# Adding gathered expert rows back: later additions for the last blocks, seven places, one rank at a time

## The chip, the cores and the metric

The kernel runs on one core of a Trainium2 chip. Its time is the device time of one execution in microseconds; before the change three runs gave a median of 1987.5 us (1986.58 to 1990.99). Engines are called by their names in the profile: PE (TensorE), PEld (TensorE's weight loads), DVE (VectorE), ACT (ScalarE), POOL (GpSimd) and SP (SyncE, which here only issues transfers).

## The reference

Two layers of cross attention and a feed-forward part run over 32 x 64 = 2048 tokens of width 512, in 32-bit floats. The change lies in the very last part, the feed-forward part of the second layer. Cut down to it:

```python
logits = x @ W_gate + b_gate                     # 8 experts
_, top_idx = jax.lax.top_k(logits, 2)
y_all = jax.nn.relu(jnp.einsum('bsd,edh->bseh', x, W_e) + b_e)   # x: layer-normed
y = jnp.take_along_axis(y_all, top_idx[..., None], axis=2)
out = x_before_norm + y.mean(axis=2)
```

Each token goes to its two best experts; the mean of the two results is added to the token.

## The kernel before

All instructions stand in one program whose order per engine is made by a scheduler from dependences, except where `pin` keeps the written order. Every engine executes its own instructions in order, and a transfer is issued by an engine's queue in order too: loads and stores of the result by SP, stores of y by ACT, gathers by POOL.

The 2048 tokens are four chunks of 512 (`NC = 4`), and each chunk is four tiles of 128 tokens (`TT = 4`), 16 tiles in all. Behind the attention, the normalised rows have been scattered into lists per expert in device memory (`xg`). The lists are worked off in blocks of 128 rows: `NB = 39` blocks, of which the first `FULL = 17` hold no row of the last chunk, and the first `COVER = 31` hold all rows of the first three chunks.

The last loop runs over `m` from 0 to 39. Round m turns block m (`block_turn`, L1445: four transposes on PE and a copy on ACT, L1447) and multiplies block m - 1 with its expert's weights (`block_expert`, products at L106). Then DVE adds the bias (L1466) out of the PSUM bank, of which there are two for these products, ACT applies Relu with a factor of one half (L1467) and stores the block's 128 rows of 512 to `yg` in device memory (L1468). The rows of a block are loaded by `load_rows` (L1426 reads a register with the place, L1431 loads), four blocks to one tile of the `t8` ring, which has four places; the last tile holds blocks 37 and 38.

From round 31 on the way back begins. `send_back(c, t)` issues two gathers (L1474, indirect transfers on POOL): for each token of tile t of chunk c its row of rank 0 and its row of rank 1, out of `yg` into a place `ys` of 2 x 512 values per partition. Five such places lie in the `weights` tile. Odd rounds send one tile, even rounds two, so the 12 tiles of the first three chunks are sent in rounds 31 to 38. These gathers need the first 31 blocks; those of the last chunk need all 39.

`combine(c, t, ys)` adds the two gathered rows (L1483), adds the sum to the tile of x (L1484), both on DVE and pinned, and stores the tile as result (L1485, SP). Odd rounds from 33 on combine one tile, even rounds two, up to round 38, which makes nine tiles (0 to 8). In a round the combine stands behind the bias addition of block m - 1. After the loop each of the last chunk's four tiles is sent, with one combine after each send, and then the rest is combined. Tiles are numbered 0 to 15 below in the order in which they are sent.

Of the kernel before, what the change touches and what calls it, by code (L numbers as in the profile page):

```python
# [12 lines left out]
ALU = mybir.AluOpType  # L13
# [16 lines left out]
def layers(ctx: ExitStack, tc: tile.TileContext, a: dict, out: bass.AP):  # L30
    nc = tc.nc
# [40 lines left out]
    def t8(name):  # L72
        return pools["work"].tile([P, 4, 512], F32, tag="t8", name=name, bufs=bufs["t8"])
# [25 lines left out]
    def pin(ins):  # L99
        return tc.keep_in_program_order(ins)  # L100
# [9 lines left out]
    weights = xpool.tile([P, 2, 5120], F32, tag="weights", name="weights")  # L110
# [182 lines left out]
    COVER = (2 * FIRST + NE * (P - 1)) // P  # L293
    NB = (2 * T + NE * (P - 1)) // P
# [491 lines left out]
    for i in range(len(order) + 1):  # L786
# [53 lines left out]
        p, step = divmod(i, 4)  # L840
# [341 lines left out]
    def attn1_out(k, oT, halves):  # L1182

        for i in halves:
            pp = ps_mm(f"pp_{k}_{i}")[:, 0:256]
            ss = slice(256 * i, 256 * i + 256)
            accumulate_next(pp, [(oT[:, j, :], wo1[:, j, ss]) for j in range(4)])
            x = xs[k][:, ss]
            nc.vector.tensor_tensor(x, pp, x, ALU.add)
# [76 lines left out]
    def route_row(c, h, at, t, r):  # L1266
        ins = pin(
            nc.gpsimd.indirect_dma_start(
                out=xg,
                out_offset=bass.IndirectOffsetOnAxis(ap=at[:, r, t : t + 1], axis=0),  # L1270
                in_=h[:, t, :],
                in_offset=None,
            )
        ).ins
        for other in sum(scatters.values(), []):
            tc.declare_no_dep(ins, other, reason="rows of a list are distinct")
        if c == NC - 1:
            for load in full_loads:
                tc.declare_no_dep(ins, load, reason="rows of full blocks are others")
        for clearing in clearings:  # L1280
            tc.add_manual_dep(ins, clearing.name, waits, reason="cleared before")
        scatters[c].append(ins)
# [138 lines left out]
    def load_rows(j0, j1):  # L1421

        base = 0 if j0 < FULL else FULL
        xr = t8(f"xr_{j0}")
        for j in range(j0, j1):
            v = nc.values_load(  # L1426
                tables[base][0:1, 1, j - base : j - base + 1], engines=[mybir.EngineType.SP],
                min_val=0, max_val=NE * T - P,
                skip_runtime_bounds_check_because="an expert's list and a block within it",
            )  # L1430
            load = nc.sync.dma_start(xr[:, j - j0, :], xg[bass.ds(v, P), :]).ins  # L1431
            for c in range(NC):
                for ins in scatters[c]:
                    if j < FULL and c == NC - 1:
                        tc.declare_no_dep(load, ins, reason="rows of full blocks are others")
                    else:
                        tc.add_manual_dep(load, ins.name, waits, reason="all rows are written")
            if j < FULL:
                full_loads.append(load)
        return xr  # L1440

    def block_turn(j, xr):
        pt = ps_tr(f"px_{j}").rearrange("p (k n) -> p k n", k=KT)
        for k in range(KT):
            pin(nc.tensor.transpose(pt[:, k, :], xr[:, k * P : (k + 1) * P], ident))  # L1445
        xT = t2(f"xT_{j}").rearrange("p (k n) -> p k n", k=KT)
        nc.scalar.copy(xT, pt)  # L1447
        return xT

    def block_expert(j, xT):  # L1450
        base = 0 if j < FULL else FULL
        v = [
            nc.values_load(
                tables[base][0:1, 0, j - base : j - base + 1], engines=[e],
                min_val=0, max_val=NE - 1,
                skip_runtime_bounds_check_because="a count of lists, less than NE",
            )
            for e in (mybir.EngineType.PE, mybir.EngineType.DVE)
        ]
        py = ps_mm(f"py_{j}")  # L1460
        flat = arena.rearrange("p e k n -> p (e k) n")
        accumulate_next(
            py, [(xT[:, k, :], flat[:, bass.ds(v[0] * KT + k, 1), :]) for k in range(KT)]
        )
        y = t2(f"y_{j}")
        pin(nc.vector.tensor_tensor(y, py, be1[:, bass.ds(v[1], 1), :], ALU.add))  # L1466
        nc.scalar.activation(y, y, AF.Relu, scale=0.5)  # L1467
        nc.scalar.dma_start(yg[j * P : (j + 1) * P, :], y)  # L1468

    def gather(c, t, at, ys):  # L1470

        slots_of = COVER if c < NC - 1 else NB
        for r in range(2):
            nc.gpsimd.indirect_dma_start(  # L1474
                out=ys[:, r, :],
                out_offset=None,
                in_=yg[0 : slots_of * P, :],
                in_offset=bass.IndirectOffsetOnAxis(ap=at[:, r, t : t + 1], axis=0),
            )

    def combine(c, t, ys):
        x = xs[c * TT + t]
        pin(nc.vector.tensor_tensor(ys[:, 0, :], ys[:, 0, :], ys[:, 1, :], ALU.add))  # L1483
        pin(nc.vector.tensor_tensor(x, x, ys[:, 0, :], ALU.add))  # L1484
        nc.sync.dma_start(out[(c * TT + t) * P : (c * TT + t + 1) * P, :], x)  # L1485

    for k in range(KT):
# [17 lines left out]
    def route_step(c, step):  # L1505
        n = f"e{c}"
        if step in ("rows0", "rows2"):
            t0 = int(step[-1])
            if t0 == 0:
                prep["h"] = route_rows if c < NC - 2 else t8(f"h_{n}")  # L1510
            stats = row_stats([xs[c * TT + t0 + i] for i in range(2)], f"{n}_{t0}")
            for i in range(2):
                norm_row(c, t0 + i, stats, prep["h"][:, t0 + i, :], i)
        elif step in ("turn0", "turn2"):
            t0 = int(step[-1])
            if t0 == 0:
                prep["fT"] = route_T if c < NC - 2 else t8(f"fT_{n}")
            for t in (t0, t0 + 1):
                turn_row(t, prep["h"][:, t, :], prep["fT"], n)
        elif step == "logits":  # L1520
            prep["parts"] = route_parts(c, prep["fT"])
        elif step == "ranks":
            prep["keep"] = route_keep(c, prep["parts"])
        elif step == "places":
            at = route_places(c, prep["keep"])
            sends.extend((c, prep["h"], at, t, r) for t in range(TT) for r in range(2))
# [99 lines left out]
    assert not sends  # L1626
    xr, turned, waiting, back = {}, None, [], 0

    def send_back(c, t):
        nonlocal back  # L1630
        ys = weights[:, 1, back % 5 * 1024 : (back % 5 + 1) * 1024]
        back += 1
        ys = ys.rearrange("p (r n) -> p r n", r=2)
        gather(c, t, slots[c], ys)
        waiting.append((c, t, ys))

# [7 lines left out]
    for m in range(NB + 1):  # L1644
        xT = turned
        if m < NB:
            if loads and loads[0][0] == m:
                j0, j1 = loads.pop(0)
                rows_m = load_rows(j0, j1)
                xr.update({j: rows_m[:, j - j0, :] for j in range(j0, j1)})  # L1650
            if m == 0:
                attn1_out(NC * TT - 1, oTs.pop(NC * TT - 1), (0, 1))
            turned = block_turn(m, xr.pop(m))
        if m > 0:
            block_expert(m - 1, xT)
        for step in between.get(m, ()):
            route_step(NC - 1, step)
        for _ in range(2):
            if sends:
                route_row(*sends.pop(0))  # L1660
        if m == 9:
            tables[FULL] = close_rest()
        elif m > 16 and m - 17 < NC:
            slots[m - 17] = token_rows(m - 17)
        if m >= COVER and left:
            for _ in range(2 - m % 2):
                if left:
                    send_back(*left.pop(0))
        for _ in range(2 - m % 2 if COVER + 2 <= m < NB else 0):
            combine(*waiting.pop(0))  # L1670
    assert not sends and not left
    for t in range(TT):
        send_back(NC - 1, t)
        combine(*waiting.pop(0))
    while waiting:
        combine(*waiting.pop(0))

# [53 lines left out]
```

## Time and profile before

| what | us |
|---|---|
| median of three runs | 1987.5 |
| the profiled execution | 1988.88 |
| its span, first to last instruction | 1987.0 |
| PE busy in the span | 1888.4 |
| DVE busy | 1056.9 |
| POOL busy | 548.3 |
| gathers (L1474), all 32: first and last start | 1930.5 and 1977.8 |
| one gather on POOL, median | 0.954 |
| from a gather's issue to its landing, least, median, most | 3.3, 5.1, 6.4 |
| one addition at L1483 or L1484 on DVE | 0.69 |
| store of a result tile to its landing, least, median, most | 2.0, 4.2, 6.8 |

In the rows of the order in time, the first number is the start in us from the span's start, the second the duration, then the engine (with a q: its queue), the line, the operation, what is written <- what is read, and in brackets how long the engine had been idle and what ended it. A row of the table of windows has the stretch, its width, then for PE, PEld, DVE, ACT and POOL the busy time and number of instructions, then the granted clock of PE (1.00 is full), the busy share of the 16 DMA engines and their GB/s.

### The profile page before, as it was taken

What the parts mean: (1) busy time and instruction counts of PE and PEld (TensorE: products, weight loads), DVE (VectorE), ACT (ScalarE), POOL (GpSimd) and SP (SyncE); (2) the same over time, 40 slices, a digit from 0 to 9 for tenths busy, and PEclk for the clock granted to TensorE, in tenths of its full rate; (3) what the DMA queues carried; (4) which work ended last, traced back from release to release, by engine and by line L of the source; (5) the groups of instructions that cost most, each with busy time, mean ns of one, the idle gap of its engine ahead of it and who ended that gap; (6) DMA issues with size and microseconds to landing.
All of it is one profiled execution on the core that took longest, in us unless ns stands there. A gap on an engine that the chain in (4) does not pass through costs nothing.

```text
span 1987.0 us, 26632 instructions
## 1 busy us (share of the span) xinstructions
PE 1888.4 (95%) x10544; PEld 1545.4 (78%) x10544; DVE 1056.9 (53%) x2077; ACT 519.9 (26%) x1019; POOL 548.3 (28%) x581
## 2 busy tenths in 40 slices
PE   7999999999998799999999999999999999879993
PEld 5888988889887698998998987787777776655441
DVE  6455445445546754454454456455466466663415
ACT  2211212212212222122122122311221565543221
POOL 7221121121322211211211211141344535540115
PEclk9999999999999899999999999999999999989997
DMA  9992110111210101111110012000004201214628
GB/s 330 307 301 89 39 43 33 33 43 40 67 43 11 43 33 32 43 32 33 43 32 22 22 59 88 19 1 11 0 22 138 64 12 54 85 71 133 217 94 271
DMA packets 129882, 151.72 MB, mean 76 GB/s; under 512 B 4704, under 2 KB 84384, under 8 KB 129760
## 3 DMA queue, kind: packets, MB, share of 16 engines
q1 hardware_dynamic: 118752, 122.70, 19.5%
q0 software_dynamic: 5392, 17.11, 2.6%
q10 hardware_dynamic: 5616, 10.23, 1.4%
q8 instruction: 84, 1.38, 0.3%
q14 instruction: 38, 0.31, 0.1%
HBM read 92.60 MB, written 56.36 MB: 75 GB/s over the span
## 4 chain that ended last, share of the span: by engine, by line
PE 88%; DVE 6%; DMA 2%; ACT 2%; issue 1%; POOL 1%; POOLq 0%; SPq 0%; DVEq 0%; ACTq 0%
PE ppx_o L464 11%; PE pqx_a L464 9%; PE sc_a L106 6%; PE pqz_a L464 6%; PE ppz_o L464 6%; PE py L106 6%; PE po_o L106 3%; PE pp L106 3%; PE pdx_f L464 3%; PE pqv_a L464 3%; PE ppy_o L464 3%; PE pqy_a L464 3%; PE px_v L554 2%; PE phx_f L464 2%; PE px_k L554 2%; PE pq_b L106 2%
## 5 line engine op out<-in xcount | busy, mean ns | idle before, releaser
L405 ACT ACTIVATE at_a<-at_a 128x512 f32<-128x512 f32 x64 | 40.4, 631 | 444.0 <-DVE at_a L404 444.0
L106 PE MATMUL py<-arena,xT 128*128 x312 | 140.8, 593 | 0.4 <-ACT xT L1447 0.2
L633 ACT ACTIVATE u_a<-pqx_a,bq 128x256 f32<-128x256 f32 x192 | 80.6, 471 | 163.4 <-PE pqx_a L464 161.1
L464 PE MATMUL ppx_o<-weights,oT_o 128*128 128x256 f32 x512 | 122.8, 383 | 0.1
L464 PE MATMUL pqz_a<-arena 128*128 128x256 f32 x512 | 121.0, 379 | 0.0
L464 PE MATMUL pqx_a<-arena,weights 128*128 128x256 f32 x512 | 121.0, 379 | 0.0
L106 PEld LDWEIGHTS sc_a<-kv,qT_a 128*128 128x128 f32 x1024 | 119.4, 192 | 1.7
L106 PE MATMUL sc_a<-kv,qT_a 128*128 128x64 f32 x1024 | 117.9, 273 | 0.0
L729 DVE TENSOR_TENSOR x<-ppx_o,x 128x512 f32<-128x512 f32 x128 | 86.9, 679 | 46.5 <-PE ppx_o L464 44.6
L464 PEld LDWEIGHTS pqz_a<-arena 128*128 128x128 f32 x512 | 97.2, 190 | 13.6 <-issue 0.4
L641 DVE TENSOR_TENSOR qT_a<-pqz_a,u_a 128x512 f32<-128x512 f32 x64 | 44.3, 692 | 113.9 <-ACT u_a L633 81.1
L464 PEld LDWEIGHTS pqx_a<-arena,weights 128*128 128x128 f32 x512 | 94.9, 190 | 12.0 <-DMA arena<-in_ctxT 0.2
L464 PEld LDWEIGHTS ppx_o<-weights,oT_o 128*128 128x128 f32 x512 | 94.8, 190 | 12.0 <-ACT oT_o L719 0.5
L106 PEld LDWEIGHTS py<-arena,xT 128*128 128x128 f32 x312 | 56.1, 190 | 56.5 <-issue 56.0
L446 POOL TENSOR_TENSOR arena<-weights 128x512 f32<-128x512 f32 x15 | 19.1, 1272 | 270.3 <-PE ppz_o L464 270.3
L436 POOL TENSOR_TENSOR arena<-weights 128x512 f32<-128x512 f32 x17 | 21.8, 1286 | 204.0 <-PE pqz_a L464 200.9
L436 POOL TENSOR_TENSOR kv_room<-weights 128x256 f32<-128x256 f32 x14 | 10.7, 762 | 238.6 <-DMA weights<-in_Wkv 238.6
L641 DVE TENSOR_TENSOR qT_a<-pqy_a,u_a 128x512 f32<-128x512 f32 x32 | 22.1, 692 | 101.5 <-PE pqy_a L464 101.5
L1466 DVE TENSOR_TENSOR y<-py,weights 128x512 f32<-128x512 f32 x39 | 26.9, 691 | 85.0 <-PE py L106 77.2
L403 DVE TENSOR_REDUCE mx_a<-sc_a 128x8 f32<-128x512 f32 x64 | 44.3, 692 | 44.3 <-PE sc_a L106 44.3
L106 PE MATMUL po_o<-atT_o,kv 64*128 64x256 f32 x512 | 65.9, 392 | 0.8 <-ACT atT_o L698 0.8
L1015 POOL TENSOR_TENSOR s_f<-s_f,arena 128x512 f32<-128x512 f32 x16 | 21.5, 1361 | 157.0 <-DVE s_f L1012 117.1
(427 smaller groups left out, 4264.9 us busy)
## 6 DMA issues: line engine op xcount, KB each, us to landing
xg<-zero SPq DMA_DIRECT2D x8, 4096.0 KB, 20.1
weights<-in_Wq SPq DMA_DIRECT2D x16, 1024.0 KB, 5.3
weights<-in_Wo SPq DMA_DIRECT2D x16, 1024.0 KB, 5.3
xr<-xg SPq DMA_DIRECT2D x39, 256.0 KB, 3.5
yg<-y ACTq DMA_DIRECT2D x39, 256.0 KB, 2.2
weights<-in_Wkv SPq DMA_DIRECT2D x16, 512.0 KB, 3.4
arena<-in_W_e SPq DMA_DIRECT2D x8, 1024.0 KB, 6.1
x<-in_x SPq DMA_DIRECT2D x16, 256.0 KB, 8.3
```

The source lines that it names most:

```text
L106: nc.tensor.matmul(ps, lhsT, rhs, start=(i == 0), stop=(i == len(pairs) - 1))
L403: nc.vector.tensor_reduce(mx, p3, AX.X, ALU.max)
L405: nc.scalar.activation(dst, dst, AF.Exp, scale=scale)
L436: engine.tensor_tensor(s1, a21, a22, ALU.add)
L446: engine.tensor_tensor(t1, b12, b11, ALU.subtract)
L464: nc.tensor.matmul(ps[:, m, :], left[:, k, m * P : (m + 1) * P], right[:, k, :], start=first and m == i == k == 0, stop=i == len(pairs) - ...
L554: nc.tensor.matmul(out_ps, *sides, start=first and m == k == 0, stop=k == 1, skip_group_check=True,)
L633: nc.scalar.activation(u[:, m * 256 : (m + 1) * 256], ps[:, m * 256 : (m + 1) * 256], AF.Identity, bias=bq[:, 4 * g + 2 * heads + m : 4 * ...
L641: nc.vector.tensor_tensor(q5[:, heads, :, 4 * half : 4 * half + 4, :], ps.rearrange("p (m b q) -> p m b q", m=2, q=64), u.rearrange("p (m ...
L729: nc.vector.tensor_tensor(dst, ps.rearrange("p (m n) -> p m n", m=2), dst, ALU.add)
L1015: nc.gpsimd.tensor_tensor(y, y, gamma, ALU.mult)
L1466: pin(nc.vector.tensor_tensor(y, py, be1[:, bass.ds(v[1], 1), :], ALU.add))
```

## The change

Three things change, all on the way back. The combines of rounds 37 and 38 leave the loop, and behind the loop all but three of the waiting tiles are combined ahead of the last chunk's gathers; the last chunk's four tiles are then sent without a combine between them. Gathered rows get seven places instead of five: two more lie in a tile of the `t8` ring, taken when the sixth tile is sent. And `combine` adds each rank's rows to x in an instruction of its own instead of adding the two ranks first.

```diff
     def combine(c, t, ys):
         x = xs[c * TT + t]
-        pin(nc.vector.tensor_tensor(ys[:, 0, :], ys[:, 0, :], ys[:, 1, :], ALU.add))
-        pin(nc.vector.tensor_tensor(x, x, ys[:, 0, :], ALU.add))
+        for r in range(2):
+            pin(nc.vector.tensor_tensor(x, x, ys[:, r, :], ALU.add))
         nc.sync.dma_start(out[(c * TT + t) * P : (c * TT + t + 1) * P, :], x)
...
+    homes = [weights[:, 1, i : i + 1024] for i in range(0, 5120, 1024)]
+
     def send_back(c, t):
         nonlocal back
-        ys = weights[:, 1, back % 5 * 1024 : (back % 5 + 1) * 1024]
+
+        if back == 5:
+            two = t8("ys").rearrange("p i n -> p (i n)")
+            homes.extend(two[:, i : i + 1024] for i in (0, 1024))
+        ys = homes[back % 7].rearrange("p (r n) -> p r n", r=2)
         back += 1
-        ys = ys.rearrange("p (r n) -> p r n", r=2)
         gather(c, t, slots[c], ys)
         waiting.append((c, t, ys))
...
-        for _ in range(2 - m % 2 if COVER + 2 <= m < NB else 0):
+
+        for _ in range(2 - m % 2 if COVER + 2 <= m < NB - 2 else 0):
             combine(*waiting.pop(0))
     assert not sends and not left
+    while len(waiting) > 3:
+        combine(*waiting.pop(0))
     for t in range(TT):
         send_back(NC - 1, t)
-        combine(*waiting.pop(0))
     while waiting:
         combine(*waiting.pop(0))
```

In the order that the scheduler makes of it, the loads of blocks 37 and 38 move behind the first store of a result tile in SP's queue, and the three bias additions of blocks 36 to 38 follow each other on DVE without an addition of gathered rows between them.

## The prediction

> **What bounds the kernel now.** I read the page first, for the stage that the change touches, then the rows of that stage in order of time, then the waits and the landing times behind them.
>
> ```profile
> span 1987.0 us, 26632 instructions
> PE 1888.4 (95%) x10544; PEld 1545.4 (78%) x10544; DVE 1056.9 (53%) x2077; ACT 519.9 (26%) x1019; POOL 548.3 (28%) x581
> ```
>
> TensorE fills the span, but the change only touches what follows it: the way back, where gathered rows are added to x. The table of windows over that stage:
>
> ```profile
> 1897.00:1930.00 33.00, 33.00 (x105) 16.34 (x104) 5.80 (x9) 8.92 (x16) 0.00 (x0) 1.00 0.23 83
> 1930.00:1957.00 27.00, 26.54 (x77) 12.23 (x75) 15.49 (x23) 7.72 (x13) 20.73 (x20) 1.00 0.86 288
> 1957.00:1987.00 30.00, 0.00 (x0) 0.00 (x0) 11.67 (x17) 0.63 (x1) 12.33 (x13) 0.55 0.70 231
> ```
>
> TensorE (first figure after the width) is done at 1957; the last 30 us hold none of it. This tail is what can shrink. VectorE, in order of time:
>
> ```profile
> 1956.26 0.69 DVE L1484 TENSOR_TENSOR x<-x,weights 128x512 f32<-128x512 f32 x1
> 1959.49 0.69 DVE L1483 TENSOR_TENSOR weights<-weights 128x512 f32<-128x512 f32 x1 [2.53 <-DMA weights<-yg,at_r]
> 1960.21 0.69 DVE L1484 TENSOR_TENSOR x<-x,weights 128x512 f32<-128x512 f32 x1
> 1960.82 0.68 DVE L1466 TENSOR_TENSOR y<-py,weights 128x512 f32<-128x512 f32 x1
> ...
> 1982.39 0.69 DVE L1483 TENSOR_TENSOR weights<-weights 128x512 f32<-128x512 f32 x1 [0.97 <-DMA weights<-yg,at_r]
> 1983.12 0.69 DVE L1484 TENSOR_TENSOR x<-x,weights 128x512 f32<-128x512 f32 x1
> ```
>
> The bias addition of the last block (L1466 at 1960.82) stands behind the ninth tile's combine, which waited 2.53 us for its rows. The block's product was ready long before:
>
> ```profile
> 1953.06 3.67 PE L106 MATMUL py<-arena,xT 128*128 x8 [0.19 <-DVE y L1466]
> ```
>
> It ends at 1956.73. GpSimd, whose queue issues all gathers:
>
> ```profile
> 1959.88 1.13 POOL L1474 DMA_INDIRECT weights<-yg,at_r  x1 [0.30 <-issue]
> 1961.31 0.95 POOL L1474 DMA_INDIRECT weights<-yg,at_r  x1 [0.30 <-issue]
> 1968.33 0.95 POOL L1474 DMA_INDIRECT weights<-yg,at_r  x1 [6.07 <-DVE x L1484]
> ...
> 1977.79 0.95 POOL L1474 DMA_INDIRECT weights<-yg,at_r  x1 [0.30 <-issue]
> ```
>
> Its queue is full from 1930.48 to 1962.26, idle for 6.07 us, then full again with the eight gathers of the last chunk. Those need every row of yg, so also block 38's. The row blames an addition, but the addition that this gather needs for its place (tile 7's) ended at 1956.95. The real releaser is block 38's store: issued at 1962.20, its landing is
>
> ```profile
> DMA to landing us min/median/max: 5.3/5.3/5.3
> ```
>
> so 1967.5, and the gather starts 0.83 us later. The path of the end is thus: y of block 38 (1960.82), Relu and store issue (1962.20), landing (1967.5), eight gathers (1968.33 to 1977.79), landing of the last (4.5 us, 1982.3), two additions (1983.81), the last store and the end (3.2 us, 1987.0).
>
> **Part 1: additions of blocks 36 to 38 ahead of the combines.** The combines of rounds 37 and 38 (tiles 6, 7, 8) move behind y of block 38; tile 9's and the later ones stand behind them in the same order as before. No instruction is added or removed. y of block 36 still stands behind the combine of tile 5: its second row was issued at 1944.78 and took 5.9 us, so 1950.7; one addition of 0.69 us instead of two, so y of 36 at about 1951.5 (1952.22 before), and the 0.19 us hold of block 38's product goes: it would end at 1956.5. I do not count these 0.2 us, for the reason in part 2, and put y of block 38 at 1956.73 + 0.1 = 1956.8: **4.0 us** earlier. Relu and issue keep their 1.38 us: the store leaves at 1958.2.
>
> Its landing: stores of y took 2.0 us while nothing else moved and 4.3 to 5.7 us since the gathers began. Here a rule of the Trainium skill bears ("DMA: Bandwidth & Descriptors", section "Queues, rings and completion order"): each DMA engine takes turns between the queues that have work, by packets. So the store, on ScalarE's own queue, would not stand behind a backlog of the others but pay for how many of them are busy. After the change no tile is stored between about 1952.5 and 1959.0 (two stores left in that time before, at 1954.39 and 1956.98), so SP's queue should be nearly empty when the store starts. By the row of the same store the landing is 5.3, by the rule it is between 2.0 and 4.3 while only the gathers share. From 1959.0 on, tiles 6, 7 and 8 follow each other at 1.4 us with a store each, so the cover is short: I take 5.0, nearest the rows (ends 4.3 and 5.7). It lands at 1963.2; with the 0.83 us the first gather starts at 1964.0, **4.3 us** earlier.
>
> Is GpSimd free by then? Tiles 9 to 11's gathers end at 1962.26 now. Two costs: the combines of tiles 6, 7, 8 are now back to back (six times 0.72, 1957.6 to 1961.9) beside four gathers. The rows: a gather takes 0.95 us undisturbed, and 1.13 to 1.47 where additions run beside it (1951.51: 1.47). The rule speaks against the change more strongly ("SBUF — State Buffer", "Who interferes with whom"): a VectorE instruction with two inputs in SBUF, as every one of these additions, contends with a GpSimd instruction that reads SBUF, and the loser of the port blocks for the other's whole length; the page infers that writing descriptors alone is spared. Taken at its worst that is 0.69 us a gather, 2.8 us for four, and GpSimd free at 1965.0, one microsecond too late. By the rows it is four times 0.35, free at 1963.7, just under the store's landing. I take the rows; the rule's end is in the range.
>
> **Part 2: seven places.** Gathers 5, 6, 12 and 13 go to a new tile of the t8 ring. Places: tile 12 needs tile 5's combine, 13 tile 6's, 14 tile 7's (done about 1960.4), 15 tile 8's (1961.9), all ahead of 1964. So part 1 can put the combines back without stalling the gathers; with five places tile 12 would have had to wait for tile 7. Before tile 11 the places cost nothing: GpSimd's idle time before gathers was 0.3 us each, its own issue.
>
> The ring has four places, and the new tile takes one. The loads of blocks 37 and 38 (last of the ring) now wait for block 28's transposes instead of block 24's, and in SP's queue they now stand behind the first store of the result, as the listing of the program's order shows. What is moved, then, is two loads of 256 KB:
>
> ```profile
> 1895.25 1.16 SPq L1431 DMA_DIRECT2D xr<-xg  x2
> 1938.05 0.35 SPq L1485 DMA_DIRECT2D out<-x  x1
> ...
> 1944.96 0.60 PE L1445 MATMUL px<-ident,xr 128*128 128x128 f32 x4
> ```
>
> They were issued at 1895, in quiet; now behind a store at about 1937.4 (one addition earlier than 1938.05), so at 1938.2 and 1939.0 (0.83 us apart, as in back-to-back loads). Loads of this kind landed in 2.6 to 4.5 us; stores and gathers at 1938 to 1943 took 3.8 to 6.4. With 5.5 block 37's rows are there at 1943.7, needed by the transposes at 1944.96: 1.2 us to spare, block 38's (1944.5 against 1948.83) have 4. I price this at zero, hidden under the products of blocks 34 and 35; without that cover each microsecond past 1944.96 is a microsecond on the end, because block 38's product follows. At 6.4 nothing is lost yet. The 0.52 MB also come into a stretch where the DMA engines are 0.9 to 1.0 busy at about 340 GB/s: 1.5 us of their time, partly in the gaps before 1942 (shares of 0.84 to 0.91). Gathers of tiles 3 to 5 may land some 0.3 to 0.6 us later and with them y of 36, whose slack is 0.7: hence the 0.2 us that I left out above.
>
> **Part 3: each rank by itself.** Still 32 additions of 0.69 us, on the same bytes. The first now waits only for the first row. Behind the last gather one addition stands instead of two: 1.42 becomes 0.69 (with its gap), **0.7 us** off the end. Elsewhere it is hidden.
>
> **The sum.** First gather of the last chunk at 1964.0 (-4.3). Eight gathers took 9.46 us from first to last start, with two stretched ones; tiles 9 to 11 are added until about 1967, so I add one stretch of 0.35: last start at 1973.8. Landing 4.5 as before (the stores of tiles 12 and 13 beside it, as now): 1978.4; one addition, 1979.15; 3.2 us to the end: 1982.35. That is some 4.6 us off the profiled span of 1987.0, whose execution took 1988.88 in all. The median of the runs is 1987.5, so **1982.9**.
>
> **Rivals.**
> - *The transfers keep most of it.* From 1942 to 1966 the DMA engines are full. If the store takes 5.7, the last gathers run into the stores of tiles 9 to 11 (0.7 more), additions stretch three gathers more than I count (1.05), and the loads are late by a little, the gain is about 2.2: 1985.3. For it: the shares near 1.0; against: 0.5 to 0.8 from 1967 on, and two stores moved later.
> - *The places do nothing, only part 3 pays.* If the first gather did wait for the addition that its row names (1968.00) and the new order kept such an addition ahead of it: 1986.8. Against: the place's addition was over at 1956.95, and the landing fits.
> - *Slower: blocks 37 and 38 are late.* Their loads stand behind the first store. Each microsecond past 1944.96 costs one; the gain is used up with a landing at 1949.6, and the time is over by 0.2% with one past 1953.6. At 1955 it would be about 1993. The longest landing of the stretch is 6.8 us, that is 1945.0; so it needs something that no row shows.
>
> **How the numbers follow.** A change of 0.2% is about what a measurement of this kernel tells from no change, 4.0 us here: faster means below 1983.5. The likeliest case (1982.9) has 0.63, most but not all of it below that line, the kept transfers 0.26, part 3 alone 0.05, late blocks 0.06. Faster 0.58 (0.05 of the likeliest case falls short of the line), same 0.35, slower 0.07 (0.01 for part 3 alone with a little lost besides). Range: low by y of 38 at 1956.6 (-4.2), landing 4.3 (-1.0), no stretches (-0.66), a last landing of 3.8 (-0.7) and -0.7: 7.3 off, 1980.2. High by the kept transfers and half the case of part 3 alone, with the median's own spread: 1987.0.
>
> **What would show it.** Right: y of block 38 at about 1956.8 directly behind its product; the idle time ahead of the last chunk's gathers down from 6.07 to about 1 to 2 us; their first at 1964; a single addition behind the last landing. Wrong: an idle TensorE at block 37's or 38's transposes, released by a load; gathers of 1.3 us and more in a row from 1957 on; a landing of block 38's store near 6 us; or the end set by another tile's rows.

## The result

The changed kernel takes 1982.69 us (median of eight runs, 1980.77 to 1987.3) against 1987.95 us before (median of eight runs). The ratio is 0.9973, with an interval from 0.9962 to 0.9984: 5.4 us saved, somewhere between 3.2 and 7.6. The forecast was 1982.9. The profiled execution took 1984.12 us, its span is 1982.2 us, 4.8 less than the 1987.0 of before.

The page and the windows over the way back, after the change (windows: stretch, width, then PE, PEld, DVE, ACT and POOL with their busy time and count, then granted clock, busy share of the DMA engines, GB/s):

```profile
span 1982.2 us, 26637 instructions
PE 1889.5 (95%) x10544; PEld 1546.5 (78%) x10544; DVE 1054.9 (53%) x2077; ACT 520.0 (26%) x1019; POOL 548.1 (28%) x581
```

```profile
1930.00:1957.00 27.00, 26.28 (x76) 12.13 (x74) 13.13 (x21) 7.68 (x13) 20.54 (x21) 1.00 0.90 313
1957.00:1987.00 30.00, 0.00 (x0) 0.00 (x0) 13.42 (x21) 0.63 (x1) 12.15 (x12) 0.59 0.66 226
```

TensorE has the same work and ends 0.45 us earlier (1956.28 against 1956.73); GpSimd issues the same gathers. What is shorter is the tail behind TensorE: the span ends at 1982.2, so the last window holds only 25.2 us of it, where it held 30.0. VectorE in order of time, after the change:

```profile
1949.52 0.69 DVE L1484 TENSOR_TENSOR x<-x,ys 128x512 f32<-128x512 f32 x1
1950.67 0.69 DVE L1484 TENSOR_TENSOR x<-x,ys 128x512 f32<-128x512 f32 x1 [0.46 <-DMA ys<-yg,at_r]
1951.77 0.69 DVE L1466 TENSOR_TENSOR y<-py,weights 128x512 f32<-128x512 f32 x1 [0.41 <-issue]
1952.82 0.69 DVE L1466 TENSOR_TENSOR y<-py,weights 128x512 f32<-128x512 f32 x1 [0.35 <-PE py L106]
1956.32 0.69 DVE L1466 TENSOR_TENSOR y<-py,weights 128x512 f32<-128x512 f32 x1 [2.81 <-PE py L106]
...
1977.30 0.69 DVE L1484 TENSOR_TENSOR x<-x,weights 128x512 f32<-128x512 f32 x1 [0.17 <-DMA weights<-yg,at_r]
1978.36 0.69 DVE L1484 TENSOR_TENSOR x<-x,weights 128x512 f32<-128x512 f32 x1 [0.37 <-DMA weights<-yg,at_r]
```

Three bias additions (L1466) follow each other, and the last two wait for their products and no longer for gathered rows. At the end one addition stands behind the last landing. GpSimd in order of time, after the change:

```profile
1957.64 0.95 POOL L1474 DMA_INDIRECT weights<-yg,at_r  x1 [0.30 <-DVE x L1484]
1958.90 0.95 POOL L1474 DMA_INDIRECT weights<-yg,at_r  x1 [0.30 <-issue]
1960.16 0.96 POOL L1474 DMA_INDIRECT weights<-yg,at_r  x1 [0.31 <-issue]
1963.21 1.35 POOL L1474 DMA_INDIRECT ys<-yg,at_r  x1 [2.09 <-DMA out<-x]
1964.86 1.41 POOL L1474 DMA_INDIRECT ys<-yg,at_r  x1 [0.30 <-issue]
...
1970.34 1.10 POOL L1474 DMA_INDIRECT weights<-yg,at_r  x1 [0.30 <-issue]
1971.74 1.29 POOL L1474 DMA_INDIRECT weights<-yg,at_r  x1 [0.30 <-issue]
1973.33 0.95 POOL L1474 DMA_INDIRECT weights<-yg,at_r  x1 [0.30 <-issue]
```

Its idle time ahead of the last chunk fell from 6.07 to 2.09 us. As before, the releaser named is the wrong one ("out<-x", a store of the result): the store meant left at 1958.39 and landed 5.3 us later, when the gather had begun. Block 38's store left at 1957.70, and its landing time is

```profile
DMA to landing us min/median/max: 4.5/4.5/4.5
```

so 1962.2, and the gather starts 1.0 us later. The waits of GpSimd's own queue, which the trace keeps, say the same: the one for block 38's store ends at 1962.25, as it ended at 1967.55 before the change (landing at 1967.48). TensorE runs the products of blocks 37 and 38 in one piece, 16 products where a hold of 0.19 us stood between them:

```profile
1949.12 7.16 PE L106 MATMUL py<-arena,xT 128*128 x16
```

The steps of the sum side by side, in us from the span's start:

| step | before | forecast | after |
|---|---|---|---|
| y of block 38 on DVE | 1960.82 | 1956.8 | 1956.32 |
| landing time of its store | 5.3 | 5.0 | 4.5 |
| first gather of the last chunk | 1968.33 | 1964.0 | 1963.21 |
| from first to last start of its eight gathers | 9.46 | 9.81 | 10.12 |
| landing time of the last gather | 4.5 | 4.5 | 4.9 |
| last landing to the end of the last addition | 1.5 | 0.75 | 0.8 |
| span | 1987.0 | 1982.35 | 1982.2 |

### The profile page after: what moved, and what is told of

It is laid out like the page before. It is cut to its first block, busy times and chain, and to the rows that moved or that the text cites. A ratio compares the mean times of both kernels' runs of the same rounds, so it can differ in the third digit from the quotient of the medians.

```text
span 1982.2 us, 26637 instructions
## 1 busy us (share of the span) xinstructions
PE 1889.5 (95%) x10544; PEld 1546.5 (78%) x10544; DVE 1054.9 (53%) x2077; ACT 520.0 (26%) x1019; POOL 548.1 (28%) x581
## 4 chain that ended last, share of the span: by engine, by line
PE 90%; DVE 6%; ACT 1%; DMA 1%; issue 1%; POOL 1%; SPq 0%; DVEq 0%; ACTq 0%; POOLq 0%
PE ppx_o L464 11%; PE pqx_a L464 9%; PE py L106 7%; PE sc_a L106 6%; PE pqz_a L464 6%; PE ppz_o L464 6%; PE po_o L106 3%; PE pp L106 3%; PE pqy_a L464 3%; PE pdx_f L464 3%; PE pqv_a L464 3%; PE ppy_o L464 3%; PE px_v L554 2%; PE phx_f L464 2%; PE px_k L554 2%; PE pq_b L106 2%
## 5 line engine op out<-in xcount | busy, mean ns | idle before, releaser
L1466 DVE TENSOR_TENSOR y<-py,weights 128x512 f32<-128x512 f32 x39 | 26.9, 691 | 88.4 <-PE py L106 84.1
```

## The experiments

My theory is that of the forecast, called the path below: the end is set by block 38's store, the eight gathers behind it, and what stands behind the last landing; the order pays through y of block 38, the split additions at the very end, and the places pay nothing by themselves. Two rivals stand against it: the transfers decide, so that a shorter chain gives little; or the moved loads of blocks 37 and 38 are late and cost time on TensorE. Each time is compared with the kernel before on the same chip, by its ratio; the medians of before were 1988.25 (runs 1 to 4 below), 1988.34 (runs 5 to 8) and 1993.88 (runs 9 to 12).

### 1. The order alone

```diff
-        for _ in range(2 - m % 2 if COVER + 2 <= m < NB else 0):
+        for _ in range(2 - m % 2 if COVER + 2 <= m < NB - 2 else 0):
             combine(*waiting.pop(0))
+    while len(waiting) > 3:
+        combine(*waiting.pop(0))
     for t in range(TT):
         send_back(NC - 1, t)
-        combine(*waiting.pop(0))
```

> The new order alone: combines of tiles 6 to 8 behind the bias addition of block 38, five places as before, the two ranks still added to each other first. My theory (the order carries it): about 4 us less than before, near 1983.8; block 38's bias addition at about 1956.6 on its own clock, the last chunk's first gather at about 1963.5, two additions behind the last landing. Rival (the places carry it): with five places tile 12's gather waits for tile 7's combine and tile 14's and 15's for those of tiles 9 and 10, so less than 2 us are won and the gathers of the last chunk show gaps of a microsecond or more.

Measured: 1988.93 us, ratio 0.9998 (0.9988 to 1.0008); the profiled span is 1990.7. With five places this order computes something else: tiles 11, 14 and 15 are gathered into places whose earlier rows are not added yet, and the earlier tiles' additions then use the later rows and wait for them. The order in time of VectorE shows it:

```profile
1960.38 0.69 DVE L1466 TENSOR_TENSOR y<-py,weights 128x512 f32<-128x512 f32 x1 [3.06 <-PE py L106]
...
1976.92 0.69 DVE L1483 TENSOR_TENSOR weights<-weights 128x512 f32<-128x512 f32 x1 [10.19 <-DMA weights<-yg,at_r]
```

Tile 9's first addition stands still for 10.19 us until tile 14's rows are there, and the thirteen additions behind it run up to 1987.5. So the order alone is no clean test. It taught what the places are: not a saving of stalls, as the forecast had it, but what makes the order possible at all.

### 2. Order and split ranks, without the places

```diff
-        pin(nc.vector.tensor_tensor(ys[:, 0, :], ys[:, 0, :], ys[:, 1, :], ALU.add))
-        pin(nc.vector.tensor_tensor(x, x, ys[:, 0, :], ALU.add))
+        for r in range(2):
+            pin(nc.vector.tensor_tensor(x, x, ys[:, r, :], ALU.add))
```

on top of run 1, with the same overwritten rows.

> The change without its two extra places (so the loads of blocks 37 and 38 stay early). My theory: as the changed kernel, 1982.5, or up to 0.5 us better since 0.5 MB of loads leave the busy stretch. Rival (places needed): 1984.5 or more, with gaps ahead of the last chunk's gathers that an addition ends.

Measured: 1988.08 us, ratio 0.9998 (0.9991 to 1.0005). The same as run 1, for the same reason.

### 3. Split ranks alone

The edit of run 2 on the kernel before.

> Each rank by itself, nothing else. My theory: 0.7 us at the very end, and as much again because block 38's bias addition stands behind one addition after tile 8's last landing instead of two: 1.4 us less, about 1986.5. Rival (only the last addition counts): 0.7 us less, 1987.2.

Measured: 1986.85 us, ratio 0.9990 (0.9982 to 0.9998), and a span of 1985.4. VectorE and GpSimd in order of time:

```profile
1958.93 0.69 DVE L1484 TENSOR_TENSOR x<-x,weights 128x512 f32<-128x512 f32 x1 [1.54 <-DMA weights<-yg,at_r]
1959.66 0.69 DVE L1466 TENSOR_TENSOR y<-py,weights 128x512 f32<-128x512 f32 x1
...
1981.55 0.69 DVE L1484 TENSOR_TENSOR x<-x,weights 128x512 f32<-128x512 f32 x1 [0.56 <-DMA weights<-yg,at_r]
```

```profile
1967.27 0.95 POOL L1474 DMA_INDIRECT weights<-yg,at_r  x1 [5.29 <-DMA out<-x]
```

It pays twice when it stands alone: y of block 38 stands behind one addition fewer (1959.66 against 1960.82; about half of this is tile 8's rows, which came 0.56 us earlier in this execution), and one addition fewer stands behind the last landing. Together with the order only the second is left, because y of block 38 is no longer behind an addition. The gap of 5.29 us ahead of the gathers stays, so something else must close it; run 5 tests the order.

### 4. Seven places alone

```diff
+    homes = [weights[:, 1, i : i + 1024] for i in range(0, 5120, 1024)]
...
+        if back == 5:
+            two = t8("ys").rearrange("p i n -> p (i n)")
+            homes.extend(two[:, i : i + 1024] for i in (0, 1024))
+        ys = homes[back % 7].rearrange("p (r n) -> p r n", r=2)
```

> Seven places alone, with the move of the two loads that they bring. My theory: nothing, within 0.5 us of before (1987.9), since no gather waits for a place; loads of blocks 37 and 38 land about a microsecond or two ahead of their transposes. Rival 1 (places carry it): 2 us less or more. Rival 2 (the moved loads cost): 0.5 to 2 us more, TensorE idle ahead of a transpose.

Measured: 1988.27 us, ratio 0.9993 (0.9985 to 1.0001): no difference that can be told. But the profile shows the late loads at work. TensorE in order of time:

```profile
1947.24 0.63 PE L1445 MATMUL px<-ident,xr 128*128 128x128 f32 x4 [1.54 <-DMA xr<-xg]
```

The load of block 37 left at 1939.98, behind the first store of a result, and took 7.1 us; TensorE stood still 1.54 us for it. Here the delay was hidden behind the combines (y of block 38 at 1960.59, near the 1960.82 of before). In the whole change nothing would hide it; run 8 shows that.

### 5. The order with five places, one tile left waiting

Run 1 with `while len(waiting) > 1`, so that tiles 9 and 10 are added ahead of tiles 14 and 15. One overwriting stays: tile 11's rows go to tile 6's place, and tile 6's additions use them.

> The new order alone, put right for five places: all but one of the waiting tiles are combined before the last chunk is sent (in e1_order and e2_order_rank three were left, so that tiles 14 and 15 were gathered into the places of tiles 9 and 10 before those had been added; there the additions of tiles 9 and 10 used the rows of 14 and 15 and waited for them, which is what e1 and e2 measured). The order of additions on VectorE is that of the changed kernel; ranks are added to each other first. My theory (the order carries some 4 us): 1983.5 to 1984.5, with the first gather of the last chunk about 4 us earlier than before; places of tiles 9 and 10 come free before tiles 14 and 15 need them (at 1963 against 1966, and 1964.5 against 1969). Rival (seven places are needed): gathers 14 and 15 wait for additions, a microsecond or more each, 1986 or more.

Measured: 1985.28 us, ratio 0.9986 (0.9979 to 0.9992). Now the order pays 2.8 us (1.6 to 4.2) on the 1988.34 of this chip, less than the 3.8 to 4.8 that I had expected. VectorE and GpSimd in order of time:

```profile
1957.21 0.69 DVE L1466 TENSOR_TENSOR y<-py,weights 128x512 f32<-128x512 f32 x1 [3.20 <-PE py L106]
```

```profile
1963.92 0.95 POOL L1474 DMA_INDIRECT weights<-yg,at_r  x1 [0.72 <-DMA out<-x]
```

y of block 38 follows its product, and the first of the last gathers starts at 1963.92. With seven tiles to wait and five places the order is still not sound; seven places are what it needs.

### 6. The same with split ranks

> The same with each rank added by itself: the changed kernel but for its two places. My theory: 1982.7 as the changed kernel, or up to 0.5 us better since the loads of blocks 37 and 38 stay early. Rival (seven places are needed): 1985 or more.

Measured: 1984.16 us, ratio 0.9981 (0.9972 to 0.9990); tile 6 is summed as in run 5. The point estimate is 1.1 us below run 5, near the 0.7 of the forecast, but the two intervals overlap, so this run does not settle it alone. It lies 1.5 us above what I had expected. In its trace GpSimd waited 0.69 and 1.20 us ahead of tile 11's gathers, until the rows of tile 6 that they overwrite had landed, and from there on it never stood idle: its own pace, and no longer block 38's store, set the start of the last gathers. With five places part of the gain is thus lost.

### 7. The lower rows of the last chunk first

A block serves one expert and a token's two rows lie with two experts, so the lower of the two (rank 0) is never in block 38. On top of the changed kernel:

```diff
-    def gather(c, t, at, ys):
-        slots_of = COVER if c < NC - 1 else NB
-        for r in range(2):
+    def gather(c, t, at, ys, ranks=(0, 1)):
+        for r in ranks:
+            slots_of = COVER if c < NC - 1 else NB - 1 + r
...
     for t in range(TT):
-        send_back(NC - 1, t)
+        send_back(NC - 1, t, (0,))
+    for c, t, ys in waiting[-TT:]:
+        gather(c, t, slots[c], ys, (1,))
```

> The changed kernel, with the last chunk's four gathers of rank 0 sent ahead of its four of rank 1. Rank 0 is the lower of a token's two rows and no two experts share a block, so it never lies in block 38, and these four need only the first 38 blocks. My theory (the start of the last chunk's gathers is set by the landing of block 38's store, and from there GpSimd's pace sets the end): the first starts right behind tile 11's, at about 1961.4 instead of 1963.2, the gap of 2.1 us is filled, and the end comes 2 us earlier: 1980.7. Rival (the DMA engines, full until 1968, set the end): the gathers start earlier but land later, less than 0.7 us won.

Measured: 1980.62 us (1978.12 to 1983.01), ratio 0.9964 (0.9953 to 0.9975), span 1978.8: the fastest here, and 2 us below the changed kernel by the medians, though those were not measured side by side and their intervals overlap. GpSimd and VectorE in order of time:

```profile
1960.84 1.03 POOL L1474 DMA_INDIRECT ys<-yg,at_r  x1 [0.30 <-issue]
...
1970.26 0.95 POOL L1474 DMA_INDIRECT weights<-yg,at_r  x1 [0.30 <-issue]
```

```profile
1974.91 0.69 DVE L1484 TENSOR_TENSOR x<-x,weights 128x512 f32<-128x512 f32 x1 [0.19 <-DMA weights<-yg,at_r]
```

The idle time of 2.09 us is gone, but not quite as the edit is written. The scheduler put a gather of rank 1 second, and by the waits of GpSimd's queue only the first of the eight ran ahead of block 38's rows; the wait for block 38's store ended at 1962.06, just as the second could start anyway (1962.17). All 32 gathers follow each other at 0.30 us, so that GpSimd's own pace sets the end. The last start is 3.1 us earlier than in the changed kernel and the last addition 3.5 us. Of both, 1.0 us is this execution's own lead, which its first gather has already (1929.33 against 1930.37); the other 2.0 to 2.4 us fit the closed gap (1.8 us) and the 2 us between the medians. This tests the store's landing from the other side: take it off the path, and the end moves. If the transfers decided, the full DMA engines would have eaten this.

### 8. Additions without a second operand in SBUF

The operand x of the additions of tiles 6 to 14 is replaced by a PSUM bank of zeros, so these additions leave x out, and with it the rank-0 rows that the first addition put there. Same count, same place.

```diff
+            other = bank if 6 <= one < 15 else x
-            pin(nc.vector.tensor_tensor(x, x, ys[:, r, :], ALU.add))
+            pin(nc.vector.tensor_tensor(x, other, ys[:, r, :], ALU.add))
```

> The changed kernel, but the additions of tiles 6 to 14 add each gathered row to a bank of PSUM filled with zeros instead of to x (x and the first rank are left out of these tiles' results), so that they read one operand from SBUF instead of two. Waits, order and stores stay. In the traces of before and after a gather takes 0.95 us, but up to 1.47 where an addition was under way at its start or began 0.2 to 0.5 us after it. Theory 1 (an addition with two operands in SBUF holds GpSimd): all eight gathers of the last chunk take 0.95 to 1.0 us, their first to last start 8.8 us instead of 10.1, the end some 1.2 us earlier, 1981.5. Theory 2 (it is the running stores or chance): gathers of 1.1 to 1.4 us as before, the same time, 1982.7.

Measured: 1982.82 us, ratio 0.9969 (0.9958 to 0.9981). GpSimd in order of time, first and last of the last chunk's gathers, and then the waits:

```profile
1965.43 0.95 POOL L1474 DMA_INDIRECT ys<-yg,at_r  x1 [3.88 <-DMA out<-x]
...
1974.22 0.95 POOL L1474 DMA_INDIRECT weights<-yg,at_r  x1 [0.30 <-DVE x L1488]
```

```profile
PE px L1445 <- DMA xr<-xg: 1.5, 1, 1.5
```

All eight gathers last 0.95 us, none is stretched, and from first to last start it is 8.79 us against 10.12: the additions are what stretches gathers, and only with both operands in SBUF. It isn't that no addition met a gather: four of the eight began while one was under way that ended 0.27 to 0.58 us later, and earlier in the same trace, where both operands still lie in SBUF, a gather that began so took 1.45 us (at 1939.68). The median doesn't gain, against the 1.2 us that I had expected. In this execution that is so because block 37's load was late again (issued at 1939.04, landed after 7.7 us), TensorE waited 1.5 us, and y of block 38 came at 1958.65 instead of 1956.32. So the late load does reach the end in the changed kernel's own order: 1.5 of these 2.3 us are its wait, and 0.45 us this execution was behind already at block 31.

### 9 to 12. Loads early, and the places with the order

The last four ran on another chip, on which the kernel before takes 1993.88 us, some 6 us more than elsewhere; the changed kernel itself wasn't run there. Run 9 puts the two new places into the ring of small tiles, so that the loads of blocks 37 and 38 stay where they were before:

```diff
-            two = t8("ys").rearrange("p i n -> p (i n)")
-            homes.extend(two[:, i : i + 1024] for i in (0, 1024))
+            homes.extend(t4(f"ys{i}").rearrange("p a n -> p (a n)") for i in range(2))
```

> The changed kernel with its two extra places in two tiles of the t4 ring, which nothing else uses by then, instead of one tile of the t8 ring: the loads of blocks 37 and 38 stay early, as before the change. In the changed kernel's trace block 37's rows landed 1.2 us ahead of their transposes, in two variants with the same move (e4_places, e9_psum) 1.5 us too late. Theory 1 (the moved loads cost something in some executions): 0.5 to 1.5 us below the changed kernel, 1981.2 to 1982.2. Theory 2 (they are hidden, as predicted): the same, 1982.7 within 0.4 us.

Run 10 is the whole change but for the split ranks (the order and the seven places with the two additions of before).

> The changed kernel with the two ranks added to each other first: order and places without part 3. This is the least that keeps the new order right, since six tiles wait at a time in the loop and seven behind it, so fewer places are overwritten before they are added (this is also what spoiled e5 and e6: there tile 11 was gathered into tile 6's place, and tile 6's additions used tile 11's rows and waited for them). My theory: 3.5 to 4 us below before, 1984 to 1984.8; two additions behind the last landing, block 38's bias addition at about 1956.5 or, where the moved loads are late, up to 1.5 us later. Rival (part 3 carries more than its 0.7 us): 1985.5 or more.

Run 11 is run 7 with the loads of run 9.

> e7_lower_first and e8_loads_early together. My theory: 1979.5 to 1980.5, up to 1 us below e7's 1980.6. Rival (GpSimd's pace alone sets the end from 1930 on, so loads and products no longer count): as e7.

Run 12 adds to run 11 that the first two tiles' lower rows are gathered one round earlier:

```diff
+        if m == COVER - 1:
+            for _ in range(2):
+                send_back(*left.pop(0), (0,))
+        elif m == COVER:
+            for c, t, ys in waiting:
+                gather(c, t, slots[c], ys, (1,))
-        if m >= COVER and left:
+        elif m > COVER and left:
```

> e11 with the same idea at the front: the rank 0 rows of the first two tiles are gathered one block earlier (they need only 30 blocks), so that GpSimd's row of 32 gathers begins 3.9 us earlier with two of them. My theory (GpSimd's pace sets the end in e7 and e11): the first gather at about 1926, the last one's start 1.3 to 2.5 us earlier, 1978 to 1979. Rival (the DMA engines or block 38 set it): as e11.

Measured:

| run | us | ratio to before on this chip |
|---|---|---|
| 9, loads early | 1996.09 | 1.0009 (0.9999 to 1.0019) |
| 10, order and places | 1997.79 | 1.0021 (1.0013 to 1.0028) |
| 11, lower rows first, loads early | 1993.42 | 0.9998 (0.9990 to 1.0006) |
| 12, and lower rows of the first tiles | 1992.36 | 0.9990 (0.9982 to 0.9998) |

None of it is what the path expects, and run 10 is slower than before, against it. The traces show why they can't be read as tests of the edits. Run 9 on VectorE, ScalarE and TensorE in order of time:

```profile
1963.82 0.69 DVE L1466 TENSOR_TENSOR y<-py,weights 128x512 f32<-128x512 f32 x1 [9.94 <-remote]
```

```profile
1966.62 0.59 ACT L1447 COPY xT<-px 128x512 f32<-128x512 f32 x1 [13.84 <-remote]
```

```profile
1967.26 6.00 PE L106 MATMUL py<-arena,xT 128*128 x8 [11.25 <-ACT xT L1447]
```

"remote" stands where the profile finds no instruction that ended the wait. By the records block 38's transposes ended at 1951.1, and the copy that needs them came at 1966.62, after 13.84 us in which ScalarE did nothing. Block 38's rows were there, since its transposes had run. What came last is a signal from TensorE: the semaphore by which TensorE tells of finished products and transposes moved at 1963.74 and at 1966.60, right ahead of these two rows and 13.1 and 15.5 us after the recorded ends of the work that they wait for. The other three traces of this chip have such standstills too, between 1940 and 1967, on other instructions (in run 12 VectorE stands still 8.61 us ahead of y of block 34), and each ends within 0.1 us of that semaphore. No trace from elsewhere has one. Full DMA engines alone don't explain it: their busy share over the standstill of run 9 (1952.8 to 1966.6) is 0.80, and in the changed kernel's trace it is 1.04 from 1944 to 1957 without one. Whether TensorE worked later than its records say, or only its signals were late, stays open, and so does the cause; also whether the kernel before has it there, whose 6 us more would fit, and whether run 10's loss is more than its share of it. Within this chip run 11 lies 2.7 us below run 9, which fits what lower rows first gave in run 7 and proves no more. The price of the late loads thus stands on runs 4 and 8 alone, and a version with lower rows first and early loads was not measured without a standstill.

## Why the prediction was right, and where its steps were off

**The path and part 1: right.** The forecast took block 38's store, not the addition that the row named, as the releaser of the last gathers. The waits of GpSimd's queue show it in both traces, and run 7 from the other side: with a gather ahead that doesn't need block 38, the gap is gone. Run 5 shows that the order carries it, run 3 that the split alone doesn't close the gap. y of block 38 came 4.5 us earlier, against 4.0: the 0.2 us of the vanished hold, left out for the loads' sake, did come, and this execution is 0.15 us ahead already at block 31 (1929.58 against 1929.73). The rest is 0.1 us by which the two products are shorter in one piece (7.16 us, against 3.60 and 3.67), and the 0.1 us that I had put between the product's end and the addition, where the trace has 0.04.

**The store's landing: taken 0.5 us too long.** Between the row of before (5.3) and the cited rule of taking turns among busy queues (2.0 to 4.3, an estimate from the rows) I took 5.0, on the ground that the cover was short. It took 4.5, 0.2 over the rule's upper end. The quiet on SP's queue was as forecast: no store of the result left between 1951.39 and 1958.39, and block 38's store left at 1957.70 inside it. That this quiet is what shortens the landing fits the other runs but was not tested by itself: with the order of before the store landed after 4.7 to 5.4 us (before, runs 3 and 4), with the new order after 3.7 to 4.9 (after, runs 1, 2 and 5 to 8). The busy share of the DMA engines doesn't tell the landing: it was 0.98 from 1957 to 1963 here, with 4.5 us, and 0.86 from 1961 to 1968 before the change, with 5.3.

**Gathers beside additions: the size was off, and in both places.** I charged 0.35 us to each of the four gathers beside the combines that are put back. Three of them are in the rows above, 0.95 us each, and the fourth (1956.38) took 0.95 as well: the cost was nothing. The rule of the Trainium skill ("SBUF — State Buffer", "Who interferes with whom"), which I took at its worst at 0.69 us a gather, was further off as a size. But of the last chunk's eight, four were stretched (1.35, 1.41, 1.10, 1.29), where I had counted three: 10.12 us from first to last start against 9.81. The mechanism is shown by run 8 (none stretched when one operand is in PSUM); what I had missed is that it goes by the moment at which a gather starts and not by the number of additions, as the last section says. That the four cost nothing was luck: each addition beside them began behind a gather's start or ended within 0.13 us of it. GpSimd was free by 1961.1, a microsecond before the store's landing, so that this step did not decide.

**Part 2: the price right here, the reason wrong.** The moved loads cost nothing in the changed kernel's trace: issued at 1937.98 and 1939.06, landed after 5.6 and 7.4 us at 1943.5 and 1946.5, needed at 1944.82 and 1948.69. The 1.2 us to spare of the forecast were 1.3. SP's queue, after the change:

```profile
1937.01 0.35 SPq L1485 DMA_DIRECT2D out<-x  x1
1937.98 1.41 SPq L1431 DMA_DIRECT2D xr<-xg  x2
```

But the cover is thin. In runs 4 and 8 the first store left one to two us later, the load took over 7 us, beyond the 6.8 that I had called the longest of the stretch, and TensorE stood still 1.5 us. So the slower rival named the true weak point and was wrong in its size: it needs a landing of some 11 us to use up the gain (1949.6 less 1938.2), and the longest seen is 7.8 (block 38's in run 8). As to the reason, "with five places tile 12 would have had to wait for tile 7" misses the point. That wait would have cost nothing: in run 5 tile 7's additions were over at 1961.8, ahead of the landing of block 38's store (1962.9). What five places can't do is hold the rows of tiles 6, 9 and 10 until they are added: runs 1, 2, 5 and 6 show that tiles 11, 14 and 15 overwrite them (in runs 5 and 6 tile 11 alone), since a gather is ordered only behind what stands ahead of it in the program.

**Part 3: right.** One addition behind the last landing; last landing to the end of the last addition fell by 0.7 us. Run 3 measured 2.0 us (0.4 to 3.6) for it alone, of which the part through y of block 38 (1.16 us) is not to be had twice.

**The sum.** Off the span by forecast: 4.0 + 0.3 + 0 - 0.35 + 0 + 0.7 = 4.65. By the trace: 4.5 (y of block 38) + 0.8 (landing) - 0.2 (landing to start: 1.0 us, not 0.83) - 0.66 (gathers) - 0.4 (last landing 4.9) + 0.7 = 4.74, with the end's rounding 4.8. Two gains were half a microsecond larger than forecast and three losses 0.2 to 0.4 us larger. That the total is nearer than its parts is luck. The rival in which the transfers keep most named two of its terms rightly (gathers stretched, last landing longer), but they cost 0.7 us together beyond the forecast. That only part 3 pays is refuted by run 5, where the order pays without it.

## What to carry to other kernels

Where an engine's tail begins with a transfer of late results, put the last producer's instruction ahead of everything on its engine that waits for other transfers, and then ask which of the consumers don't need that last result: they can fill the landing time (some 2 us more in run 7). Whoever reorders reads and writes of reused places must count how many are alive at once: the program orders a write only behind the reads that stand ahead of it, so too few places give wrong values. A buffer taken from a ring may move an unrelated load behind a store in another queue; compare its issue, landing and need in more than one execution before it is priced at nothing.

## What the runs showed of the hardware

A gather takes 0.95 us on GpSimd, and one kind of addition on VectorE stretches it. If an addition with both operands in SBUF has begun 0.05 us or more before the gather starts, and ends more than about 0.13 us after that start, the gather ends 0.83 us after the addition does: in the changed kernel additions ending 0.27, 0.39, 0.52 and 0.58 us after the gather's start gave 1.10, 1.22, 1.35 and 1.41 us. An addition that begins after the gather's start doesn't stretch it, and here the expectation of run 8 was wrong: before the change the gather at 1950.25 took 0.95 us with an addition from 1950.73, and the changed kernel's at 1967.83 took 0.95 us with one from 1968.24. In all traces of this case 31 gathers met an addition that began 0.25 to 0.5 us after their start with none under way before it to stretch them, and all 31 took 0.95 or 0.96 us. Where a stretched gather seems to end with a later addition, that one merely follows the first back to back. An addition that reads one operand from PSUM does nothing of the kind: in the changed kernel the gather at 1956.38 took 0.95 us beside a bias addition from 1956.32. So ten additions back to back can leave every gather at 0.95 us, as in the changed kernel, or make most of them 1.02 to 1.04, as in run 7, by how the two rhythms meet.

The rule cited above agrees with this as to the two inputs in SBUF. It infers that writing descriptors is spared; the gathers here are stretched, but a gather also reads its row numbers (`at_r`) out of SBUF, and no run here tells which of the two is held.

The time from issue to landing of one and the same 256 KB load of block 37 went from 5.6 to 7.7 us between executions, with its issue only 1 to 2 us later in the stretch: 1937.98 gave 5.6, 1939.04 gave 7.7, 1939.98 gave 7.1. The moment of issue alone doesn't set it: 1937.52, in run 7, gave 6.2.

One chip took 6 us more for the kernel before than the others, and its four traces hold standstills of ScalarE or VectorE of 8 to 15 us, which end with a signal from TensorE long after the recorded end of its work; their cause was not found.
